# A graph-attention kernel: mask loads as 32-bit words on the sync queue, and a new order of units in the first and last batches

## The chip, the cores and the metric

One core of a Trainium2 chip runs the whole kernel. The metric is the device time of one launch in microseconds. Five engines matter: TensorE (PE; its weight loads are shown as PEld), VectorE (DVE), ScalarE (ACT), GpSimd (POOL) and SyncE (SP), which here only issues DMAs. Each engine executes its instructions strictly in the order in which the program gives them, and waits where an operand is not ready or a buffer is not free.

## What is computed

x is (16, 1024, 256) f32, adj is (16, 1024, 1024) int32 of zeros and ones. Two layers follow each other for each of the 16 batches; each is a pre-norm graph attention with a residual:

```python
h = jnp.maximum(_layernorm(x, axis=-1), 0.0)
x = x + _L0_gnn_ref(h, adj, ...)      # 4 heads of 64
h = jnp.maximum(_layernorm(x, axis=-1), 0.0)
x = x + _L1_gnn_ref(h, adj, ...)      # 8 heads of 32, biases on q, k, v

# inside a layer
scores = jnp.einsum('bhne,bhme->bhnm', Q, K) * scale
scores = jnp.where(adj > 0, scores, -jnp.inf)     # one mask for all heads
attn = jax.nn.softmax(scores, axis=-1)
out = concat_heads(attn @ V) @ Wo.T + bo
```

Everything is f32 on the chip.

## The kernel before, in words

Scores are computed transposed, keys on partitions and queries in columns, without subtracting a maximum; the sums of the exponentials are checked at the end (`test`, L288), and a flag computed from that check (`verdict`, L823) decides whether a slow, careful program runs instead. It does not run here.

**Steps.** The work is a list of 768 steps. A batch has two query halves (qh) of 512 queries. In layer 0 a half has two groups (pairs of heads) of 4 steps, in layer 1 two groups (four heads each) of 8 steps: 16 steps of layer 0 and 32 of layer 1 for a batch. A step is four 128 x 512 blocks. `scores` (L446) puts them on PE into two PSUM pairs out of a ring of three; `exponentials` (L461) masks each pair on DVE (L477) and takes the exponential on ACT (L483); `weigh` (L488), two steps later, multiplies by v on PE (L495). The list interleaves batches: layer 0 of batch b+1 (its first step is called a, `first[b+1]`) and then layer 1 of batch b (its first step is c = a + 16, `second[b]`).

**Order.** `Stream.run` (L541) writes every engine's program. In layer 0 it takes two steps at a time, in layer 1 one: scores of the new steps; then `weigh` of the steps two back and, in layer 1, their counting (`count_steps`); then counts that are due; exponentials; then the functions that are due at this step, first those without much PE work, last `turn`, `k`, `q`, `values`, `end_half`. `later(i, f)` makes f due at step i. All due steps are written out by hand (L766 to L819 and `end_group`), and functions that are due at one step go in the order in which they were entered; those of the hand-written list are entered before those of `end_group`.

**Sums.** In layer 0 `add_tiles` (L500) adds the exponentials' tiles on DVE and POOL (L504, L507, L508, L510). In layer 1 POOL adds the tiles of odd steps to those of even ones (L608), and `accumulate` (L591) adds two of the results by a DMA that POOL issues. `count` (L342) sums over the partitions with a matmul on ones, into a PSUM tile pz with one buffer. Then, some steps apart: `spread` (an ACT copy, L366, and four DMAs), `invert` (a DVE reciprocal and a DMA to DRAM, vd), `fetch` (DMAs back, inv), `normalize` (POOL, L406) and `end_half` (PE with wo, then x is added on DVE, L441; in layer 1 the result goes out, L444).

**Inputs.** `open_x` loads a half of x on SP into one of three buffers. `stats` (DVE), then two small POOL ops, `norm` (ACT, L214) and a transposition: for the first inputs `turn` on PE with the identity (L236), later `turn_blocks` (DVE, L240), `put_blocks` and `place_blocks` (SP, through DRAM). `k`, `q` and `values` are PE projections with a copy on ACT, DVE and ACT. `add_bias` (POOL, L223) adds the output's bias to x.

**Mask.** A batch's mask is 8 units of 128 queries x 1024 keys. `load` (L143) is a DMA on POOL's queue that turns int32 into bf16 (256 KB), into one of two buffers; `put` (ACT, L164) writes it as fp8, `flip` (DVE, L170) transposes it in 32 x 32 blocks. Four units are one half, and the first masking op of a half needs all four. `second` (ACT, L175) changes a unit for layer 1. For batch 0 the units are loaded into two tiles of the ring of the exponentials.

**Head and tail.** Before the first step the program loads weights and x, and does for both halves of batch 0 statistics, norm, turn, k, q, values, and four units of the mask (L676 to L717). At the end `finish` (L408) normalizes and writes the last half; six checks (L292) and `verdict` follow.

## Time and profile before

| what | us |
|---|---|
| median of three timed runs (3191.0 to 3192.33) | 3191.39 |
| the profiled execution's own time | 3184.43 |
| its span | 3182.7 |
| PE busy / DVE / ACT / POOL | 3119.6 / 2521.7 / 2236.4 / 2540.5 |
| adj loads: 128 issues on POOL, each on the engine | 1.62 |
| first scores of step 0 start at | 37.7 |
| step 16 / step 32 / step 64 start at | 116.7 / 210.0 / 333.5 |
| one batch in the middle (48 steps) | 194 |

A line of the timeline gives start, length, engine, line of the code, operation, what is written from what, how many, and in brackets the idle time of the engine before it with what ended it. A line of the waits gives engine and line, what was waited for, and us in total, number of times, and the longest.

### The profile page before, as it was taken

To read this page: it belongs to the slowest core of one execution; us is meant where nothing else is said; L and a number is where in the kernel's file an instruction comes from. 1 tells how busy PE (TensorE), PEld (TensorE's weight loads), DVE (VectorE), ACT (ScalarE), POOL (GpSimd) and SP (SyncE) were. 2 spreads that over 40 slices of the span, in tenths; PEclk is the share of its full clock that TensorE was granted. 3 is DMA by queue.
4 is the path that set the end of the run, shared out by engine and by line. 5 is a ranking of instruction groups with operands and counts; after the bars stand their busy time and mean duration, and the time that the engine had idled before them with its cause. 6 is when DMAs were issued, how large, how long until landed. Compare 5 with 4: busy or idle time off the path is not lost.

```text
span 3182.7 us, 45121 instructions
## 1 busy us (share of the span) xinstructions
PE 3119.6 (98%) x16662; PEld 1221.8 (38%) x16662; DVE 2521.7 (79%) x2882; ACT 2236.4 (70%) x2440; POOL 2540.5 (80%) x1358
## 2 busy tenths in 40 slices
PE   8989999999999999999999999999999999999998
PEld 3433333434334343333433334333343433434332
DVE  6678788887878878788887878878888787887776
ACT  5657767686676766767677686776768667676765
POOL 5568788797887978878788797878879788796776
PEclk9999999999999999999999999999999999999999
DMA  7216556364563745636355463555636446372421
GB/s 94 34 31 123 105 103 115 76 130 91 104 117 80 132 85 104 126 83 126 85 110 113 89 122 82 113 104 104 115 76 130 91 102 118 83 132 68 87 61 32
DMA packets 449684, 308.46 MB, mean 97 GB/s; under 512 B 248752, under 2 KB 408752, under 8 KB 432432
## 3 DMA queue, kind: packets, MB, share of 16 engines
q0 software_dynamic: 283344, 173.82, 33.8%
q1 hardware_dynamic: 166112, 131.68, 15.1%
q8 instruction: 133, 2.18, 0.3%
q14 instruction: 95, 0.78, 0.1%
HBM read 149.95 MB, written 47.96 MB: 62 GB/s over the span
## 4 chain that ended last, share of the span: by engine, by line
PE 79%; DMA 8%; DVE 7%; issue 2%; SPq 1%; POOL 1%; ACT 1%; DVEq 0%; POOLq 0%; ACTq 0%
PE ps L454 27%; PE po L495 23%; PE pq L270 11%; PE py L436 7%; PE pv L306 6%; PE pz L347 4%; DMA p<-p 4%; DVE p L477 3%; DMA out_dram<-x 3%; DMA x<-in_x_dram 1%; POOL p L608 1%; DVE p L507 1%; DVE st L195 1%; DVE p L504 1%; SPq L444 1%
## 5 line engine op out<-in xcount | busy, mean ns | idle before, releaser
L483 ACT ACTIVATE p<-p 128x1024 f32<-128x1024 f32 x1536 | 1613.0, 1056 | 722.0 <-DVE p L477 662.1
L477 DVE SCALAR_TENSOR_TENSOR p<-mask,ps 128x1024 f32<-128x1024 fp8e5 x1536 | 1786.2, 1214 | 373.8 <-PE ps L454 360.0
L608 POOL TENSOR_TENSOR p<-p,p 128x1024 f32<-128x1024 f32 x510 | 1217.8, 2449 | 135.9 <-PE po L495 115.8
L454 PE MATMUL ps<-qT,kT 32*128 32x512 f32 (+1 forms) x6144 | 1125.3, 628 | 19.7 <-DVE p L477 15.9
L495 PE MATMUL po<-p,v 128*32 128x512 f32 (+1 forms) x6144 | 981.0, 600 | 3.1 <-ACT cat L358 2.8
L454 PEld LDWEIGHTS ps<-qT,kT 32*128 32x128 f32 (+1 forms) x6144 | 380.8, 184 | 694.9 <-issue 288.8
L495 PEld LDWEIGHTS po<-p,v 128*32 128x32 f32 (+1 forms) x6144 | 233.6, 118 | 684.6 <-issue 468.2
L508 POOL TENSOR_TENSOR p<-p 128x1024 f32<-128x1024 f32 x128 | 302.5, 2363 | 89.0 <-DVE p L507 83.6
L507 POOL TENSOR_TENSOR p<-p,p 128x1024 f32<-128x1024 f32 x64 | 150.7, 2355 | 200.1 <-DVE p L504 120.3
L406 POOL TENSOR_TENSOR cat<-cat,inv 128x512 f32<-128x512 f32 x127 | 193.0, 1566 | 91.9 <-DMA inv<-vd 89.8
L270 PE MATMUL pq<-hT,wk 128*128 128x512 f32 x512 | 238.4, 609 | 2.7 <-DMA hT<-turned 1.6
L306 PE MATMUL pv<-wv,hT 128*128 128x256 f32 x1024 | 237.8, 385 | 0.1
L270 PE MATMUL pq<-hT,wq 128*128 128x512 f32 x512 | 236.6, 605 | 0.1
L436 PE MATMUL py<-wo,cat 128*128 128x256 f32 x1008 | 234.0, 385 | 1.2 <-DVE p L477 1.2
L306 PEld LDWEIGHTS pv<-wv,hT 128*128 128x128 f32 x1024 | 189.4, 190 | 72.1 <-DVE p L477 25.0
L436 PEld LDWEIGHTS py<-wo,cat 128*128 128x128 f32 x1008 | 186.6, 190 | 73.3 <-issue 35.1
L149 POOL DMA_DIRECT2D adj<-in_adj_dram x128 | 207.6, 1622 | 4.6 <-issue 4.0
L504 DVE TENSOR_TENSOR p<-p 128x1024 f32<-128x1024 f32 x128 | 171.0, 1336 | 0.0
L347 PE MATMUL pz<-p,ones 128*32 128x512 f32 x1248 | 163.4, 596 | 7.6 <-DMA p<-p 6.8
L592 POOL DMA_DIRECT2D p<-p x133 | 121.8, 916 | 53.1 <-POOL p L608 19.5
L441 DVE TENSOR_TENSOR x<-py,x 128x1024 f32<-128x1024 f32 x63 | 76.9, 1221 | 101.7 <-PE py L436 100.7
L223 POOL TENSOR_TENSOR x<-x,bo 128x1024 f32<-128x1024 f32 x64 | 156.9, 2512 | 0.0
(51 smaller groups left out, 1750.9 us busy)
## 6 DMA issues: line engine op xcount, KB each, us to landing
p<-p POOLq DMA_DIRECT2D x133, 1024.0 KB, 8.1
adj<-in_adj_dram POOLq DMA_DIRECT2D x128, 256.0 KB, 9.7
turned<-hn SPq DMA_DIRECT2D x58, 512.0 KB, 3.5
hT<-turned SPq DMA_DIRECT2D x232, 128.0 KB, 5.3
x<-in_x_dram SPq DMA_DIRECT2D x128, 128.0 KB, 2.8
inv<-vd SPq DMA_DIRECT2D x128, 128.0 KB, 2.9
inv<-vd SPq DMA_DIRECT2D x252, 64.0 KB, 4.8
out_dram<-x SPq DMA_DIRECT2D x124, 128.0 KB, 2.8
```

Source lines behind the costliest of these rows:

```text
L149: nc.gpsimd.dma_start(at, rows[u // 4, u % 4])
L270: nc.tensor.matmul(pq[:, m, :], wt[self.layer][:, c, ts(m, P)], self.hT[half][:, c, :], start=(c == 0), stop=(c == 1),)
L306: nc.tensor.matmul(pv[:, i, :], self.hT[half][:, c, ts(i, P)], w.v[self.layer][:, c, :], start=(c == 0), stop=(c == 1),)
L347: nc.tensor.matmul(self.s[ts(r, 32), :], w.ones.to_broadcast([P, 32]), of, start=start, stop=stop)
L436: nc.tensor.matmul(py[:, i, :], self.half.cat[:, c, ts(i, P)], w.o[self.layer][:, c, :], start=(c == 0), stop=(c == 1),)
L454: nc.tensor.matmul(st.ps[i // 2][:, i % 2, :], gr.inp.kT[r * D : (r + 1) * D, gr.g, ts(kt, P)], gr.inp.qT[gr.qh][r * D : (r + 1) * D, gr.g ...
L477: nc.vector.scalar_tensor_tensor(out=half, in0=gr.mask.m[gr.qh][:, kt // 4, :, kt % 4].unsqueeze(1).to_broadcast([P, 2, 512]), scalar=-EDG ...
L483: nc.scalar.activation(half, half, AF.Exp, scale=gr.scale)
L495: nc.tensor.matmul(gr.o[r * D : (r + 1) * D, :], gr.inp.v[:, kt, h * D : (h + 1) * D], st.halves[i // 2][:, i % 2, :], start=(kt == 0), st ...
L504: nc.vector.tensor_add(a, a, b)
L508: nc.gpsimd.tensor_add(a, a, b)
L608: nc.gpsimd.tensor_add(half, half, of)
```

## The change

1. `Mask.load` is issued on SP, into an int32 tile (512 KB); the mask buffers are one instead of two (the same bytes). `put` reads int32. Loads, puts and flips come at other steps: four units of a batch in the layer-0 steps a+8 to a+14, one at a+45, three at the beginning of the next 16 steps; a load stands directly behind the put of the unit before it; a flip two steps behind its put (one for unit 4).
2. Head: the identity is multiplied 16 times by itself into a PSUM tile that nobody reads. SP's order is x, wk and wq, x, four mask units, wv, four units, x of batch 1, the other weights. The steps begin after k and q of the first half, turn of the second and the first four mask units; k(1), values(0) and values(1) come at step 0, q(1) at step 2, add_bias at 10 and 12.
3. The inputs of batch 1 are due at slightly other steps, the second half of x of batch b+2 is opened at c (before at a+14), and its first statistics are at c+2 (before at c).
4. The first group of layer 1 accumulates at once instead of two steps later.
5. Last batches: other steps for `second`, for the inputs of the last layer, and for the first count of the last batch; the two tests that were at the very end come seven steps (or 37) after their group.
6. The two small tiles of `verdict` come from the pool of constants instead of a pool opened at the end.

```diff
-    adjp = ctx.enter_context(tc.tile_pool(name="adjp", bufs=2))
+    adjp = ctx.enter_context(tc.tile_pool(name="adjp", bufs=1))
...
-                at = adjp.tile([P, 4, 256], BF16, tag="adj", name=f"adj_{self.b}_{u}")
+                at = adjp.tile([P, 4, 256], I32, tag="adj", name=f"adj_{self.b}_{u}")
...
-            nc.gpsimd.dma_start(at, rows[u // 4, u % 4])
+            by.dma_start(at, rows[u // 4, u % 4])          # by=nc.sync
...
-                    self.later(i + 2, gr.count, one, j == 1, st.last)
+                    self.later(i + (4 if j == 1 and not (gr.qh or gr.g) else 2), gr.count, one, j == 1, st.last)
...
-                    if gr.qh or gr.g:
-                        self.accumulate(one, gr.one)
-                    else:
-                        self.due.setdefault(i + 2, []).insert(0, (self.accumulate, (one, gr.one)))
+                    self.accumulate(one, gr.one)
...
-                self.later(i + k if gr.inp.b + gr.layer < B - 1 else len(self.steps) + 2, gr.inp.test)
+                self.later(i + k, gr.inp.test)
...
+    warm = psum_pair("warm")
+    for _ in range(16):
+        nc.tensor.matmul(warm[:, 0, :P], w.ident, w.ident, start=True, stop=True)
+    open_w(2)
+    open_x(0, 1)
+    for u in range(4):
+        load(u)
+    open_w(1)
+    for u in range(4, NT):
+        load(u)
+    open_x(1, 0)
+    open_w(6)
+    open_x(1, 1)
+    open_w(len(loads))
     inp.stats(0)
     inp.norm(0, whole=True)
     inp.stats(1)
     inp.turn(0)
+    inp.norm(1, whole=True)
+    mask.put(0)
     inp.k(0)
+    mask.put(1)
     inp.q(0)
     inp.turn(1)
+    for u in range(4):
+        if u > 1:
+            mask.put(u)
         mask.flip(u)
...
+    for i, f, half in (0, inp.k, 1), (0, inp.values, 0), (0, inp.values, 1), (2, inp.q, 1):
+        later(i, f, half)
+    for half in range(QH):
+        later(10 + 2 * half, inp.add_bias, half)
...
-        for i, u in zip((0, 1, 2, 3, 4, 6, 8, 10), range(NT)):
+        for i, u in zip((0, 2, 4, 6, 7, 9, 11, 13), range(NT)):
             later(a + i, masks[b].second, u)
...
-            later(a + 14, open_x, b + 2, 1)
+            later(c, open_x, b + 2, 1)
...
-                norms(other, 1, c, c + 4, c + 5, c + 6, bias=c + 36)
+                norms(other, 1, c + 2, c + 4, c + 5, c + 6, bias=c + 36)
...
-            for i, t in zip((9, 13, 17, 22, 33, 37, 41, 45), range(NT)):
-                later(a + i - 5, mask.load, t)
-                later(a + i, mask.put, t)
-                later(a + i + 1, mask.flip, t)
+            at = 6, 8, 10, 12, 14, 45, 49, 51, 53
+            for t in range(NT):
+                later(a + at[t], mask.load, t)
+                later(a + at[t + 1], mask.put, t)
+                later(a + at[t + 1] + (1 if t == 4 else 2), mask.flip, t)
...
-            block_inputs(last, 0, c + 10, c + 11, c + 12, c + 14, c + 16, c + 20)
-            norms(last, 1, c + 13, c + 14, c + 16, c + 17)
-            block_inputs(last, 1, c + 18, c + 19, c + 20, c + 24, e + 6, e + 4)
-            for u in range(NT):
-                later(c + 8 + 2 * u, masks[b + 1].second, u)
+            block_inputs(last, 0, c + 10, c + 11, c + 12, c + 16, c + 20, c + 24)
+            norms(last, 1, c + 13, c + 16, c + 20, c + 21)
+            block_inputs(last, 1, c + 22, c + 23, c + 24, c + 28, e + 8, e)
+            for i, u in zip((4, 5, 8, 12, 16, 20, 24, 28), range(NT)):
+                later(c + i, masks[b + 1].second, u)
...
-    row = work.tile([P, 1], F32, tag="row", name="row")
+    row = w.row
...
-    bad = work.tile([1, 1], I32, tag="bad", name="bad")
+    bad = w.bad
```

(e = c + 32 is the first step of the last batch's layer 1.)

## The prediction

> **What bounds the kernel now.** I read the page first, then PE's waits, over the whole span and over the long middle, then timelines where these waits fall.
>
> ```profile
> PE 3119.6 (98%) x16662; PEld 1221.8 (38%) x16662; DVE 2521.7 (79%) x2882; ACT 2236.4 (70%) x2440; POOL 2540.5 (80%) x1358
> ...
> PE 79%; DMA 8%; DVE 7%; issue 2%; SPq 1%; POOL 1%; ACT 1%; DVEq 0%; POOLq 0%; ACTq 0%
> ```
>
> TensorE is the bound, and the change removes no matmul. Only 3182.7 - 3119.6 = 63 us of idle PE (and a few us at a low clock) can be won. PE's waits (us in total, times, longest), whole span:
>
> ```profile
> PE ps L454 <- DVE p L477: 15.9, 18, 2.1
> PE ph L236 <- ACT hn L214: 13.2, 5, 10.3
> PE pz L347 <- DMA p<-p: 6.8, 13, 1.2
> PE tot L831 <- DVE row L829: 6.4, 1, 6.4
> PE po L495 <- ACT cat L358: 2.8, 3, 2.2
> ...
> PE pq L270 <- DMA hT<-turned: 1.6, 1, 1.6
> ```
>
> and between 260 and 3120 us:
>
> ```profile
> PE ps L454 <- DVE p L477: 9.8, 14, 0.8
> PE pz L347 <- DMA p<-p: 6.8, 13, 1.2
> ```
>
> So a batch in the middle (194 us) loses just two stalls, 0.75 and 0.52 us. With a the first layer-0 step of a batch and c = a + 16, the first sits at step c+3 and the second at c+11, in each of 13 batches. The timeline of the first, in batch 3:
>
> ```profile
> 800.47 1.75 SPq L135 DMA_DIRECT2D x<-in_x_dram  x4
> 802.26 0.43 SPq L389 DMA_DIRECT2D vd<-vn  x1
> 804.70 0.43 DVE L195 BATCH_NORM_STATS2 st<-x 128x6 f32<-128x256 f32 x1 [2.11 <-DMA x<-in_x_dram]
> 808.84 3.91 POOL L406 TENSOR_TENSOR cat<-cat,inv 128x512 f32<-128x512 f32 x2 [5.74 <-DMA inv<-vd]
> 809.51 2.11 DVE L507 TENSOR_TENSOR p<-p,p 128x1024 f32<-128x1024 f32 x1
> 812.80 1.13 PE L454 MATMUL ps<-qT,kT 32*128 32x512 f32 x4 [0.74 <-DVE p L477]
> ```
>
> The x load of step a+14 holds SP 6.3 us, until 800.47 (SP's own waits name the out DMA of that buffer). The normalizer's vd, ready at 797.0, queues behind it; POOL gets inv 5.74 us late; its multiply then lies on top of DVE's L507, which takes 2.11 us where it takes 1.23 alone (at 748.84); the next masking op frees its PSUM pair late. Head and tail:
>
> ```profile
> 10.26 2.80 PE L236 MATMUL ph<-ident,hn 128*128 128x128 f32 x8 [10.26 <-ACT hn L214]
> 14.16 5.56 PE L270 MATMUL pq<-hT,wk 128*128 128x512 f32 x8 [1.10 <-ACT hT L237]
> 19.55 3.60 PE L270 MATMUL pq<-hT,wq 128*128 128x512 f32 x8
> 54.20 1.13 PE L454 MATMUL ps<-qT,kT 64*128 64x512 f32 x4 [2.01 <-DVE p L477]
> 3175.74 0.22 DVE L829 TENSOR_REDUCE row<-chk 128x1 f32<-128x64 f32 x1 [3.40 <-DMA out_dram<-x]
> ```
>
> **Head.** Until 24.0 us PE does the same work in the same order: turn(0), k(0), q(0), turn(1), here without values(0) between. First the masks: SP now issues eight 512 KB loads behind x, wk, wq, x. In 0:40 the hardware queue moved 4.46 MB in 53% of 40 us, 210 GB/s; seven half-MB transfers to the fourth mask end near 2 + 17.5 = 19.6 us, the first mask at 12. ACT's order is norm(1) to 16.2, put(0) 1.15 to 17.4, kT copy 19.75-20.8, put(1) to 21.9, hT copy (1.0) after turn(1), 25.1, put(2), put(3) to 27.4; DVE flips the last (0.45) by 28.0. So no mask load is late, and the first masking op (L477) starts at 28.0 instead of 38.9. PE meanwhile waits: 0.4 for the qT copy (23.2 + 1.2), then three score pairs fit PSUM and the fourth waits from 27.65 to 29.2, 1.55; together 2.0. k(1), values(0), values(1) follow at 30.4 (10.3 us, covering DVE and ACT, which finish at 34), scores of steps 2 and 3 at 40.7, and from there PE has q(1) and the projections of batch 1 to put beside DVE. Before, the stretch after 37.7 lost 0.8 (8.10 for 32 score matmuls against 2 x 3.63), 2.01, 1.04 (0.45, 0.16, 0.43) and 1.7 (clock 0.50 for 3.41 us at 55.5), 5.5. Gain 5.5 - 2.0 = 3.5. From below: all of 5.5; from above: a loss of 3, if DVE still falls behind and the clock halves again (2.0 + 1.7 more than taken).
>
> The 16 identity matmuls: a 128x512 product is two rows of 0.45, so a 128-column one is 0.22, 16 are 3.5 us at full and 7 at half clock. They start when the identity is made, 1.5, end by 8.5, and PE idles to 10.26 as before. The 2.01 us idle above was enough for the clock to halve, so I take 0; if the clock held, 0.8 of turn(0) (its last rows come from ACT at 11.7) and 2.1 of the k group would go, -2.9.
> The Trainium skill ("TensorE: Matmul & The Clock Gate", Part 1) has a free-running activity window of some 3.4 us: a mostly idle window halves the clock. By it the 1.8 us or more to 10.26 lose the warmth in some window phases and keep it in others, 0 or -2.9; the 3.41 us at 0.50 in this trace agree with the window's length.
>
> **Batches 0 and 1 (80-265 us), 12 us of stalls.** Two stalls of 0.26 and 0.43 at 193-195 us come from a mask put ahead of the kT copy (192.9); it moves one due slot earlier and clears, -0.7. The 1.19 at 265 is POOL's queue: adds, accumulate, two multiplies, add_bias, adds; the bias (2.4) moves 30 steps on and the mask load issue (1.6) leaves: -1.2. A flip (0.43) joins the overloaded DVE at a+7: +0.4. The 2.1 us stalls at 160, 208 and 217 have their causes (statistics, qT copy, norm) left where they are. Net -1.5, between -4 and +3.
>
> **Middle, 13 batches.** (1) x half 1 opens at c instead of a+14, statistics at c+2. In SP's place now stands mask load 4, which waits for put(3) on ACT. The exponentials end at 797.7, put at 798.8, so vd goes at 799.3 instead of 802.3, less some 1 to 2 us for following half a MB. DVE's 2.11 wait goes. L507 then meets the multiply wholly, partly or not; of 0.75 I take 0.45, ends 0 and 0.75. (2) The accumulate of the first layer-1 group is issued with its adds (end 829.9), not behind the next adds (837.9). Landing takes 8.1, so it is there at 839 for a count at 846: all of 0.52 goes. POOL idles 829.9-833.3, so the issue (0.9) is free. (3) 8 loads a batch leave POOL, 8 x 1.62 = 13 us, and enter SP, 8 x 0.45 of issue, SP being mostly idle. POOL is not the bound: 0 itself. (4) Puts and flips: the same number, moved. ACT's tight iterations gain 1.05 each: 6-7 has 1.6 us free before its next exponential, 10-11 1.67, 14-15 1.66. DVE's flip at a+7 takes 0.35 of 0.92 free; at a+3 and a+5 there are 1.7 and 3.6. So 0, held for +0.15 a batch. (5) SP's order: each load t+1 stands behind put t, at the end of an ACT iteration; sums wait for ACT's copy anyway; the fetch at a+8 starts some 3 us later, its multiply at 775.8 moves to about 778, before the next POOL add at 780.2. One buffer instead of two: a load has an iteration (7.2 us or more). (6) put now reads four bytes an element; ACT's exponential reads f32 in 1.06 for as many columns, put takes 1.14 from bf16, so 1.14 stays. In DMA time a load falls: 8 loads were 72.2% of 40 us in the head (3.6 us each on all engines), on the hardware queue 0.52 MB at 210 GB/s is 2.5; DMA was 50% busy, so 0. Sum 13 x (0.45 + 0.52 - 0.15) = 10.7, between -16.5 and +6.
> The Trainium skill ("DMA: Bandwidth & Descriptors", Queues, rings and completion order) speaks against (5): descriptors of one queue are taken in ring order, so small vd and inv transfers now wait behind mask bytes that lay on another queue. No row before shows it; with 210 GB/s it would be 2.5 us on a chain that has won 3, and (1) would give 0: 13 x 0.45 = 6 us less gain.
>
> **Last batch, 5.4 us of stalls** (2.22, 1.56, 0.20, 0.21, 0.44, 0.80 between 2976 and 3077). The second mask pass (1.1 on ACT each) starts four steps earlier and is spread; k, q, v of half 0 go 2 to 4 steps later, so hT (late by 1.56) is there; the first pair's count goes two steps later, past the copy of the sums it waited 0.80 for. The moved projections (k(1), q(1), v(1)) are PE work either way. I take -3.5, ends 0 and -5.4.
>
> **Tail.** row and bad leave a pool that took over the x buffer: L829 no longer waits for the out DMA. Four of six L292 (0.24 each) go earlier, so bad is done at 3172.3, not 3176.43. Then loads of the flag (0.5), PE's branch (4.37) and 1.1 of ending follow: 3178.6 for 3182.7, -4.1. SP issues out DMAs to 3174.1 and has its own chain of about 3.5, ending 3177-3178, just beside. Ends -1 and -4.5.
>
> **Sum**, against the profiled execution (3184.43: span 3182.7 and 1.7 around it): -3.5 - 1.5 - 10.7 - 3.5 - 4.1 = -23.3, 3161.1. The median of the runs, 3191.39, is 7.0 above the profiled one; the same gain gives **3168.1**.
>
> **Rivals.** (B) The middle's stalls stay or others of the same size replace them: only ends gain, -12.6, 3179. For: L507 is late by overlap, which a 2 us shift may not end; against: the second stall has a plain cause. (C) The clock holds from the identity matmuls and the middle wins both stalls: -30, 3161. (D) Slower: mask load 0 lands late. It is issued near 763.9, behind x and beside hT; put(0) stands in ACT ahead of the po copy (L358), which PE needs at 775.2. Up to 9.6 us of landing cost nothing, then PE loses one for one in each of 14 batches; (23.3 + 6.4)/14 = 2.1, so it decides from 11.7 us. At 12.5 it costs 41 us, 3209. For: mask loads landed in 9.7 on POOL's queue (18.5 in the head); against: 512 KB of turned on SP lands in 3.5. (E) No change to be measured: new ACT, DVE or SP lateness of about 1.5 us a batch, 3188. For: 70 to 98% full iterations in layer 0.
>
> **Numbers.** Forecast 0.47 (3158 to 3177), C 0.10, B 0.18, E 0.13, D 0.12. Faster by over 0.2% (6.4 us, about what a measurement can tell from none): 0.75; within: 0.13; slower: 0.12. The range leaves out D and the tips: 3158 to 3191.
>
> **What would show it.** First L477 near 28 us; k matmuls after 14 us at 0.85 or 0.45 each (clock); the waits of PE without "pz <- DMA p<-p" and with "ps <- DVE p" under 8 us; vd issued before x at c; L829 without a DMA wait. Wrong: ACT's put (L164) waiting for "DMA adj" in layer 0, new stalls repeated every 194 us.

## The result, and the profile after

The changed kernel takes 3428.22 us (median of four runs, 3419.01 to 3435.93) where the kernel before takes 3191.19 (3190.60 to 3192.33): 1.074 times as long, with a 95% interval of 1.071 to 1.077. I had forecast 3168.1 and a range up to 3191. The profiled execution of the changed kernel has a span of 3417.2 us, 234.5 more than the 3182.7 before.

The page of the changed kernel, the line of busy times and the chain of work that ended last (shares by engine, then by line):

```profile
PE 3191.7 (93%) x16694; PEld 1243.8 (36%) x16694; DVE 2531.5 (74%) x2882; ACT 2236.8 (65%) x2440; POOL 2311.5 (68%) x1230
...
PE 53%; DMA 26%; SPq 6%; DVE 6%; POOL 4%; issue 3%; ACT 3%; DVEq 0%; POOLq 0%; ACTq 0%
PE ps L456 17%; PE po L497 15%; DMA adj<-in_adj_dram 10%; PE pq L272 8%; PE py L438 7%; DMA vd<-vn 6%; DMA p<-p 4%; DVE p L479 4%; PE pz L349 3%; PE pv L308 3%; POOL p L610 2%; DMA inv<-vd 2%; DMA x<-in_x_dram 2%; SPq L137 2%; DMA sums<-s 1%
```

TensorE was 79% of the chain and DMA 8%; now they are 53% and 26%, and one tenth of the span is the mask's loads. PE's idle time went from 63.1 us to 225.5 (+162.4), and its busy time rose by 72.1 although only the 16 small products were added. Most of that second part is the clock. The trace's clock records (each gives a stretch and the share of TensorE's full clock granted in it) have 196.6 us at half clock, before 23.1, and PE was busy for 137.4 us of that, before for 10.3; half of this difference is 63.6 us, and the products took some 6. Idle and busy time together are the 234.5. The two largest waits of PE, and the mask's line of ACT's waits, in the changed kernel (engine, line, what was waited for; us in total, times, longest):

```profile
PE ps L456 <- ACT v L312: 90.3, 13, 8.5
PE ps L456 <- DVE p L479: 49.7, 20, 8.9
```

```profile
ACT mask L166 <- DMA adj<-in_adj_dram: 326.0, 96, 10.8
```

and the same line in the kernel before:

```profile
ACT mask L164 <- DMA adj<-in_adj_dram: 3.7, 1, 3.7
```

Before, ACT waited for a mask load once, now 96 of 128 times. It is the sign that the prediction named for being wrong. Where it hurts is seen in the timeline of batch 3 (its a begins at 768.1), SP's queue first, then ACT, then PE:

```profile
816.28 0.63 SPq L151 DMA_DIRECT2D adj<-in_adj_dram  x1
821.31 1.21 SPq L391 DMA_DIRECT2D vd<-vn  x1
827.46 0.61 SPq L151 DMA_DIRECT2D adj<-in_adj_dram  x1
```

```profile
826.28 1.15 ACT L166 ACTIVATE mask<-adj,numbers 128x1024 fp8e5<-128x1024 int32 x1 [6.77 <-DMA adj<-in_adj_dram]
827.34 0.57 ACT L360 COPY cat<-po 128x512 f32<-128x512 f32 x1
827.80 1.15 ACT L177 ACTIVATE mask<-mask,numbers 128x1024 fp8e5<-128x1024 fp8e5 x1
828.85 1.00 ACT L312 COPY v<-pv 128x1024 f32<-128x1024 f32 x1
...
837.93 1.15 ACT L166 ACTIVATE mask<-adj,numbers 128x1024 fp8e5<-128x1024 int32 x1 [1.95 <-DMA adj<-in_adj_dram]
```

```profile
823.43 1.99 PE L456 MATMUL ps<-qT,kT 64*128 64x512 f32 x8
829.90 2.08 PE L456 MATMUL ps<-qT,kT 64*128 64x512 f32 x4 [4.48 <-ACT v L312]
```

Mask load 0 is issued at 816.28 and `put` starts with it at 826.28, 10.0 us later. ACT stands idle for 6.77 of these. Behind the put in ACT's order lie the copy of po, a second mask pass and, last, the copy of v out of PSUM (the memory that PE writes to); the next scores need that PSUM pair and wait 4.48 us. The clock records have half clock from 829.88 on, for 3.41 us. `put` empties the one buffer, so load 1 goes at 827.46, and its put starts 10.5 us later: the loads alternate with the puts, one after another.

Time between the starts of the steps' scores, mean of 12 middle batches, worked out from the trace (a is the first layer-0 step, c = a + 16; only rows that differ by over 0.3 us somewhere; the other kernels are those of the experiments):

| steps | before | after | load in four parts | before, x at c | last kernel |
|---|---|---|---|---|---|
| a+2 to a+4 | 10.85 | 12.07 | 10.85 | 10.85 | 10.85 |
| a+4 to a+6 | 11.99 | 15.20 | 11.99 | 11.99 | 11.99 |
| a+10 to a+12 | 7.22 | 16.78 | 8.23 | 7.22 | 7.22 |
| c to c+2 | 9.36 | 9.78 | 9.36 | 9.36 | 9.36 |
| c+2 to c+4 | 9.81 | 7.65 | 7.66 | 7.72 | 7.66 |
| c+4 to c+6 | 8.64 | 13.23 | 8.67 | 8.64 | 8.70 |
| c+6 to c+8 | 8.40 | 7.63 | 7.63 | 7.63 | 7.63 |
| c+10 to c+12 | 6.10 | 5.36 | 5.36 | 6.07 | 5.36 |
| c+12 to c+14 | 7.65 | 8.26 | 8.24 | 7.65 | 8.21 |
| whole batch | 194.41 | 210.38 | 192.37 | 191.51 | 191.36 |

The places of loss in "after" are those of the mask: the puts of units 6 and 7 (steps a+3 and a+5), put(0) at a+8, which stops a+10, and c+4, where x is late. There the mask's load is the cause at one remove. In batch 4, SP's queue:

```profile
1071.04 0.62 SPq L151 DMA_DIRECT2D adj<-in_adj_dram  x1
1071.76 1.87 SPq L391 DMA_DIRECT2D vd<-vn  x1
1079.67 2.42 SPq L400 DMA_DIRECT2D inv<-vd  x4
1082.18 1.95 SPq L137 DMA_DIRECT2D x<-in_x_dram  x4
```

vd is 8 KB, but its readers wait until 1079.67, 6 us after its issue has ended; x stands behind them, DVE's statistics wait for x until 1087.07, and the scores wait 1.34 us for DVE. Over the whole run SP waited for vd 318.5 us in 54 places (5.9 each), before 160.3 in 84 (1.9 each).

**How fast is such a load?** A stretch of the changed kernel's trace in which nothing but one mask load is in flight, 840.5 to 846.5 us (packets, megabytes, share of 16 engines):

```profile
DMA packets 484, 0.49 MB, mean 82 GB/s; under 512 B 1, under 2 KB 484, under 8 KB 484
...
q1 hardware_dynamic: 484, 0.49, 25.1%
```

25.1% of 16 engines are 4.02 engines: one load is served by four engines, at 82 GB/s, however idle the others are. 0.52 MB take 6.4 us at that rate; from the issue to a put that waits for it pass 8.2 us at the least and 10.0 in the median of the 96. The load's source is written with four dimensions, `k r g c`, and k, the slowest, has 4 values.

The Trainium skill ("DMA: Bandwidth & Descriptors", "Why a DMA increments its semaphore by 16 and not by 1") has a rule that fits: a DMA uses the largest number of engines, up to 16, that divides the slowest dimension of both its sides; with 4 and 128 that is 4. The trace's 4.02 agrees.

### The profile page after: what moved, and what is told of

Read it like the earlier page. It is cut to its first block, busy times and chain, and to the rows that moved or that the text cites. A ratio compares the mean times of both kernels' runs of the same rounds, so it can differ in the third digit from the quotient of the medians.

```text
span 3417.2 us, 45104 instructions
## 1 busy us (share of the span) xinstructions
PE 3191.7 (93%) x16694; PEld 1243.8 (36%) x16694; DVE 2531.5 (74%) x2882; ACT 2236.8 (65%) x2440; POOL 2311.5 (68%) x1230
## 4 chain that ended last, share of the span: by engine, by line
PE 53%; DMA 26%; SPq 6%; DVE 6%; POOL 4%; issue 3%; ACT 3%; DVEq 0%; POOLq 0%; ACTq 0%
PE ps L456 17%; PE po L497 15%; DMA adj<-in_adj_dram 10%; PE pq L272 8%; PE py L438 7%; DMA vd<-vn 6%; DMA p<-p 4%; DVE p L479 4%; PE pz L349 3%; PE pv L308 3%; POOL p L610 2%; DMA inv<-vd 2%; DMA x<-in_x_dram 2%; SPq L137 2%; DMA sums<-s 1%
## 5 line engine op out<-in xcount | busy, mean ns | idle before, releaser
L456 PE MATMUL ps<-qT,kT 32*128 32x512 f32 (+1 forms) x6144 | 1163.6, 640 | 174.0 <-ACT v L312 90.3
L408 POOL TENSOR_TENSOR cat<-cat,inv 128x512 f32<-128x512 f32 x127 | 166.2, 1314 | 327.0 <-DMA inv<-vd 296.0
L166 ACT ACTIVATE mask<-adj,numbers 128x1024 fp8e5<-128x1024 int32 x128 | 146.8, 1148 | 326.0 <-DMA adj<-in_adj_dram 326.0
L438 PE MATMUL py<-wo,cat 128*128 128x256 f32 x1008 | 247.3, 401 | 7.7 <-DVE p L479 7.5
L438 PEld LDWEIGHTS py<-wo,cat 128*128 128x128 f32 x1008 | 196.0, 200 | 92.3 <-DVE p L479 31.9
L506 DVE TENSOR_TENSOR p<-p 128x1024 f32<-128x1024 f32 x128 | 198.0, 1547 | 0.9 <-PE po L497 0.9
L349 PE MATMUL pz<-p,ones 128*32 128x512 f32 x1248 | 170.8, 617 | 24.3 <-DMA p<-p 24.3
L197 DVE BATCH_NORM_STATS2 st<-x 128x6 f32<-128x256 f32 x256 | 108.2, 423 | 92.1 <-DMA x<-in_x_dram 87.6
L443 DVE TENSOR_TENSOR x<-py,x 128x1024 f32<-128x1024 f32 x63 | 77.2, 1225 | 122.7 <-PE py L438 122.5
```

Of the source, the lines that this page charges most:

```text
L349: nc.tensor.matmul(self.s[ts(r, 32), :], w.ones.to_broadcast([P, 32]), of, start=start, stop=stop)
L408: nc.gpsimd.tensor_mul(o, o, inv)
L438: nc.tensor.matmul(py[:, i, :], self.half.cat[:, c, ts(i, P)], w.o[self.layer][:, c, :], start=(c == 0), stop=(c == 1),)
L456: nc.tensor.matmul(st.ps[i // 2][:, i % 2, :], gr.inp.kT[r * D : (r + 1) * D, gr.g, ts(kt, P)], gr.inp.qT[gr.qh][r * D : (r + 1) * D, gr.g ...
L506: nc.vector.tensor_add(a, a, b)
```

## The experiments

Theory A: the load is slow because it is one DMA on four engines; all else follows from puts that wait. Rivals: it is slow because it shares SP's queue with other transfers (B), or because it is int32, twice the bytes (C), or because of one buffer or the order of loads and puts (D).

### The load in four parts

```diff
-            by.dma_start(at, rows[u // 4, u % 4])
+            for k in range(4):
+                by.dma_start(at[ts(k, 32)], rows[u // 4, u % 4][k])
```

Same bytes, queue, buffer and steps; the slowest dimension of each part is 32.

> The changed kernel with each mask load issued as four DMAs of 32 partitions (128 KB) instead of one of 128 partitions; bytes, buffers, steps and queue as they are. Theory A (few DMA engines): with nothing else in flight the load moves 81 packets of 1 KB a us at 53 ns each, so 4.3 engines work, and the outermost dimension of its source has 4 entries; with 32 entries all 16 work. Then a load lands in 3 to 4 us, ACT's wait for adj falls from 326 us to under 20, and the kernel takes 3165 to 3180 us. Theory B (one buffer and SP's order: a load stands behind the put of the unit before it and behind other transfers): the waits stay, and the time stays over 3390 us, with 384 more issues on SP.

Measured: 3158.01 us (3155.12 to 3159.24), 0.991 of the kernel before on the same chip (0.989 to 0.993), and 270 us less than the changed kernel. Its ACT wait, the landing of a part on the page, and the window 795.25 to 798, in which the parts of a load (and one 8 KB vd) are in flight:

```profile
ACT mask L167 <- DMA adj<-in_adj_dram: 25.6, 13, 2.7
```

```profile
adj<-in_adj_dram SPq DMA_DIRECT2D x512, 128.0 KB, 3.0
```

```profile
DMA packets 681, 0.52 MB, mean 190 GB/s; under 512 B 178, under 2 KB 681, under 8 KB 681
...
q1 hardware_dynamic: 681, 0.52, 61.7%
```

61.7% are 9.9 engines, 190 GB/s instead of 82. ACT's wait falls from 326.0 us to 25.6, the half-clock time from 196.6 to 32.7, PE's waits for `ACT v` are gone, and those for `DVE p` fall from 49.7 us to 10.7. Theory A stands. B, C and D alone are not enough for the loss: queue, bytes, buffer and order are those of the changed kernel.

### The same number of DMAs, but four engines each

```diff
-            by.dma_start(at, rows[u // 4, u % 4])
+            for g in range(4):
+                by.dma_start(at[:, g, :], rows[u // 4, u % 4][:, :, g, :])
```

Cut along g, so that k stays the slowest dimension.

> The same number of DMAs as in e1_split_k (four of 128 KB for a load), but cut along the other dimension: each has all 128 partitions, and the outermost dimension of its source still has 4 entries. Theory A: the same 4 engines carry all four, a load still lands in 8 to 10 us, and the time is that of the changed kernel, 3415 to 3450 us. Theory C (a single DMA of 512 descriptors is slow as such): smaller DMAs land sooner, and the time falls to that of e1_split_k.

Measured: 3328.71 us in one run (before 3188.51). The window 827 to 831 and the waits:

```profile
DMA packets 364, 0.36 MB, mean 91 GB/s; under 512 B 10, under 2 KB 364, under 8 KB 364
...
q1 hardware_dynamic: 364, 0.36, 25.6%
```

```profile
ACT mask L167 <- DMA adj<-in_adj_dram: 231.0, 71, 8.7
```

The part on the engines is right: 25.6% are 4.1 engines, so it is the shape and not the number of DMAs that decides. The time is not: it lies 140 us above before, but 100 below the changed kernel, which theory A did not expect. From the issue of a load's first part to a put that waits for it pass 9.1 us in the median, 0.9 less than in the changed kernel; SP's wait for vd is smaller (273.1 us instead of 318.5) and so is PE's for p<-p (7.5 instead of 24.3). Whether small transfers get in between the four parts wasn't tried; these 100 us stay open.

### Loads on POOL's queue again, with the new steps

```diff
-        def load(self, u, at=None, by=nc.sync):
+        def load(self, u, at=None, by=nc.gpsimd):
```

once with bf16 tiles and two buffers, as before (the lines for the tiles are left out here), and once with int32 and one buffer.

> The changed kernel with mask loads as before: bf16 on POOL's queue with two buffers; steps of loads, puts and flips, head and last batches as changed. Theories A and B: the 7% are all in the load, so the time falls to 3170 to 3185 us. If the new steps of the units themselves are at fault, it stays over 3300 us.

> The changed kernel with its 32-bit loads and its one buffer, issued on POOL's queue instead of SP's. Theory A: POOL's queue has used all engines for the same shape before (its loads of this shape did not hold ACT up), so the time falls under 3200 us although the buffer is single. Theory B (one buffer): the alternation of put and load stays and the time stays over 3300 us.

Measured: bf16 3293.06 us, 1.033 of before (1.031 to 1.035); int32 3450.5 in one run. I had expected both to be near or below the kernel before, and both are far above. The landing in the kernel before, then the lines of landing and of ACT's wait, bf16 and then int32:

```profile
adj<-in_adj_dram POOLq DMA_DIRECT2D x128, 256.0 KB, 9.7
```

```profile
adj<-in_adj_dram POOLq DMA_DIRECT2D x128, 256.0 KB, 10.9
```

```profile
ACT mask L166 <- DMA adj<-in_adj_dram: 185.8, 69, 6.3
```

```profile
adj<-in_adj_dram POOLq DMA_DIRECT2D x128, 512.0 KB, 11.6
```

```profile
ACT mask L166 <- DMA adj<-in_adj_dram: 267.0, 81, 7.4
```

So the load was never fast: POOL's loads landed in 9.7 us before, and land here in 10.9 (256 KB) and 11.6 (512 KB). That POOL's queue had used all engines, as I had assumed for the int32 kernel, no run shows. The kernel before hid it. Its loads were issued five steps ahead of the put, and the distance from issue to put was never under 11.7 us (median 17.8). With the new steps a load goes directly behind the put of the unit before it: in the bf16 kernel ACT had to wait for 69 loads, and without its wait it would have been there 9.7 us after the issue (median of the 69). Before PE loses, the order of the change leaves load 0 some 5 us (worked out below), and only a load in four parts lands in about that. Theory D is half right: with slow loads, the new order is what makes them felt.

Two more things make these kernels slow, so they are no pure test of the load. In both, POOL issues the mask loads ahead of its statistics in the head (shown in the next experiment), and step 16 starts at 134.3 and 139.0 us, against 115.0 with the four parts on SP. And with one buffer POOL itself stands at a load until the put has emptied the buffer: 268.8 us in 72 places in the int32 kernel, while the bf16 kernel's POOL waits less than 7 us ahead of its loads. What the buffer and what the bytes have of the 157 us between the two was not separated.

### POOL's loads two iterations ahead

```diff
-                later(a + at[t], mask.load, t)
+                later(a + (at[t - 1] if t else 4), mask.load, t)
```

on the bf16 kernel.

> e3_pool_bf16 (mask loads as bf16 on POOL's queue, two buffers, else as changed: 3293 us) with each load issued two iterations before its put instead of one. Theory: a load in this shape takes 9 to 11 us on either queue, and the changed order gives it one layer-0 iteration (7.2 us and more); with two it is there. ACT's wait for adj (186 us) falls under 15, and the time to 3160 to 3180. If the moved puts and flips or the loads' share of POOL are at fault, the time stays over 3270.

Measured: 3228.86 us, 1.012 of before (1.010 to 1.014). ACT's wait:

```profile
ACT mask L166 <- DMA adj<-in_adj_dram: 22.6, 6, 6.5
```

185.8 us of it went to 22.6, with the same slow loads, and 64 us of time with it: the lead is what counts. But I had expected it below the kernel before, and it is 38 above. The step table names two places. One is the head: step 16 starts at 133.3 us instead of 116.7. No put there waits for a load. POOL does its work in order, and its small statistics op stands behind all eight load issues:

```profile
3.58 9.22 POOL L151 DMA_DIRECT2D adj<-in_adj_dram  x6
18.26 1.54 POOL L151 DMA_DIRECT2D adj<-in_adj_dram  x1 [5.46 <-issue]
19.82 1.05 POOL L205 TENSOR_TENSOR rstd<-ve,numbers 128x4 f32<-128x4 f32 x1
```

DVE's part for it was ready at 8.23; so PE's first transposition starts at 21.84 instead of 10.26. The other place is a+14 to a+16, 10.77 us instead of 7.22 in each batch, where PE's scores wait for DVE's addition of x (L443, 27.3 us in 14 places). In batch 3 POOL's multiply waits 5.06 us for inv, until 814.61; POOL's adds come behind it, DVE's masking op waits 7.91 us for them, and x's addition stands behind that. Why inv is late in this kernel I have not settled.

### The identity matmuls: none, 16 and 30

On the kernel with four parts: without the 16 products, and with 30 of them.

```diff
-    for _ in range(16):
+    for _ in range(30):
```

> e1_split_k (3158 us) without the 16 identity matmuls. In e1's trace they end at 7.6, PE is then idle for 2.5 us, the clock is halved from 9.7 to 20.0 us, and the first 8 k matmuls take 6.62 us. Theory: they win nothing; without them the clock rises within the k matmuls as before the change (full from 17.9), the first scores start at 23 to 26 us, and the time is within 3 us of e1's share of the kernel before (0.9908). Rival: they hold the clock in most executions, and without them 3 us are lost.

> e1_split_k with 30 identity matmuls instead of 16, so that they last to where the first transpositions start (10 to 11 us). Theory: without the idle 2.5 us the clock stays full from about 6 us on, the first 8 k matmuls take 3.6 to 3.8 instead of 6.62 us, the first scores start at 21.5 to 23 instead of 25.5, and the kernel gains 2 to 3 us on e1. Rival: the clock halves all the same, and only PE's queue gets longer (0 to +1 us).

Measured: none 3154.96 us, 0.989 of before (0.987 to 0.990); 30 3150.45, 0.987 (0.986 to 0.989); 16 had 0.991 (0.989 to 0.993). Step 16 starts at 114.1, 111.5 and 115.0 us. The timelines of the head, with 16 and with 30 (three groups each):

```profile
1.54 6.09 PE L686 MATMUL warm<-ident 128*128 128x128 f32 x32 [1.54 <-POOL ident masks.py:199]
10.13 2.80 PE L239 MATMUL ph<-ident,hn 128*128 128x128 f32 x8 [2.50 <-ACT hn L217]
14.04 6.62 PE L273 MATMUL pq<-hT,wk 128*128 128x512 f32 x8 [1.10 <-ACT hT L240]
```

```profile
1.54 9.91 PE L686 MATMUL warm<-ident 128*128 128x128 f32 x60 [1.54 <-POOL ident masks.py:199]
11.29 1.05 PE L239 MATMUL ph<-ident,hn 128*128 128x128 f32 x8
13.44 3.70 PE L273 MATMUL pq<-hT,wk 128*128 128x512 f32 x8 [1.10 <-ACT hT L240]
```

With 16, PE idles 2.50 us before the first real work, the clock records show half clock from 9.7 to 20.0 us, and the products with wk take 6.62 us, longer than the 5.56 of the kernel before. With 30 the clock does not fall in the head, they take 3.70, and the first scores start at 22.0 instead of 25.5. Sixteen products win nothing; what counts is that they reach up to the real work.

The Trainium skill ("TensorE: Matmul & The Clock Gate", Part 1) gives a window of about 3.4 us after which the clock is set; the records at half clock here are 3.41 us long and multiples of it, except where a program ends in one, which agrees. The page speaks of an idle window; here PE was busy for 1.32 of the 3.41 us before 9.72, and for 1.40 of those before 55.48 in the kernel before, and the clock halved both times.

### One part of the change alone: x opened at c

The kernel before, with two lines of part 3 only:

```diff
-            later(a + 14, open_x, b + 2, 1)
+            later(c, open_x, b + 2, 1)
...
-                norms(other, 1, c, c + 4, c + 5, c + 6, bias=c + 36)
+                norms(other, 1, c + 2, c + 4, c + 5, c + 6, bias=c + 36)
```

> The kernel before with one part of the change: the second half of x of batch b+2 is opened at c instead of a+14, and its first statistics are at c+2 instead of c. Prediction's step: SP no longer stands at that x load while vd waits, so the steps c+2 and c+3 of a middle batch (9.81 us together before, 7.66 in e1_split_k) fall to 9.0 or less, and 13 batches win 6 to 28 us; the stall of pz at c+11 may stay. If the stall comes from the overlap of DVE and POOL alone, the two steps stay at 9.8.

Measured: 3147.14 us in one run, 44 below the 3190.70 of the kernel before on that chip; the middle gains 2.90 us a batch (c+2 to c+4 2.09, c+6 to c+8 0.77). In this kernel's SP queue vd and inv go ahead of x:

```profile
792.96 0.34 SPq L389 DMA_DIRECT2D vd<-vn  x1
796.67 2.40 SPq L398 DMA_DIRECT2D inv<-vd  x4
799.19 1.95 SPq L135 DMA_DIRECT2D x<-in_x_dram  x4
```

and the scores of c+3 come without a wait:

```profile
807.88 1.22 PE L454 MATMUL ps<-qT,kT 32*128 32x512 f32 x8
```

The same group in the kernel before:

```profile
812.80 2.26 PE L454 MATMUL ps<-qT,kT 32*128 32x512 f32 x8 [0.74 <-DVE p L477]
```

Only 0.74 of what was lost there stood in the idle list; another 1.04 stood inside the busy time of that group, whose second half waited too, and 0.77 came at c+6. My prediction had read 0.75 from the idle column. This one part gives 0.986 of the kernel before in its one run, and the last kernel below, with every part and fast loads, 0.984: nearly all that was won here lies in these two lines.

### One part alone: accumulating at once

The kernel before, with part 4 only:

```diff
-                    if gr.qh or gr.g:
-                        self.accumulate(one, gr.one)
-                    else:
-                        self.due.setdefault(i + 2, []).insert(0, (self.accumulate, (one, gr.one)))
+                    self.accumulate(one, gr.one)
```

> The kernel before with one part of the change alone: the first group of layer 1 accumulates at once instead of two steps later. My prediction's step (2): PE's wait for the DMA that accumulates (6.8 us in 13 places) goes and nothing takes its place, the steps c+10 to c+14 take together 13.0 to 13.3 us instead of 13.75 and the time is some 6.8 us less, about 3182. Theory from the run with the mask loads in four parts: the counts only move, steps c+10 to c+12 fall from 6.10 to 5.36 and c+12 to c+14 rise from 7.65 to about 8.2, a batch loses 0 to 0.2 us less, and the time is the same within 3 us.

Measured: 3189.29 us in one run, against 3189.63. c+10 to c+12 falls from 6.10 to 5.36 and c+12 to c+14 rises from 7.65 to 8.12; the batch is 194.36 instead of 194.41. Of the 0.74 won, 0.47 is lost again at the next steps, as the second theory has it; another 0.33 comes at c+2 (10.14 instead of 9.81), which it had not foreseen and which I have not traced. Nothing is won.

### One part alone: the verdict's tiles

The kernel before, with part 6 only (`row = w.row`, `bad = w.bad`).

> The kernel before with one part of the change alone: the two small tiles of the flag's computation come from the pool of constants. My prediction's step (tail, ends -1 and -4.5): L829 has no DMA wait and PE's branch comes earlier; the four early tests are not in this kernel, so the part is at most 3.4 us, the wait of L829 on the out DMA before, and the stretch from the last step's scores to the end falls from 29.1 to about 25.7 us; everything before it stays, 3188. Rival: the program ends with SP's chain (its last out DMA issue at 3174.1 and about 3.5 us behind it), so less than 1.5 us of that is seen, and the stretch stays above 27.6.

Measured: 3181.09 us in one run, against 3189.63. From the last scores to the end 24.5 us instead of 29.1. The checks of the sums end at 3172.21 in this kernel; DVE's next row:

```profile
3172.24 0.22 DVE L830 TENSOR_REDUCE row<-chk 128x1 f32<-128x64 f32 x1
```

The reduction follows the checks at once, where it waited 3.40 us for the out DMA before. The tail's gain of the whole change, 3.8 to 3.9 us, is no larger than this part's, 4.6. The 1.2 us beyond the wait come from the clock: in the kernel before a half-clock record of 3.41 us begins at 3165.0 and the last 14 products with wo take 4.95 us; here no such record lies there, and they take 3.60.

### The last batch, and the first half of x

The four-part kernel lost 3.4 us between step 704 and the last step's scores where I had forecast a gain of 3.5. On the kernel with 30 products, the last batch's order of before was put back (steps of the last inputs, of `second` and of its first count):

```diff
-                    self.later(i + (4 if j == 1 and not (gr.qh or gr.g) else 2), gr.count, one, j == 1, st.last)
+                    self.later(i + 2, gr.count, one, j == 1, st.last)
...
-            block_inputs(last, 0, c + 10, c + 11, c + 12, c + 16, c + 20, c + 24)
-            norms(last, 1, c + 13, c + 16, c + 20, c + 21)
-            block_inputs(last, 1, c + 22, c + 23, c + 24, c + 28, e + 8, e)
-            for i, u in zip((4, 5, 8, 12, 16, 20, 24, 28), range(NT)):
-                later(c + i, masks[b + 1].second, u)
+            block_inputs(last, 0, c + 10, c + 11, c + 12, c + 14, c + 16, c + 20)
+            norms(last, 1, c + 13, c + 14, c + 16, c + 17)
+            block_inputs(last, 1, c + 18, c + 19, c + 20, c + 24, e + 6, e + 4)
+            for u in range(NT):
+                later(c + 8 + 2 * u, masks[b + 1].second, u)
```

and a second kernel has besides

```diff
-            later(a + 6, open_x, b + 2, 0)
+            later(a + 7, open_x, b + 2, 0)
```

so that mask load 0 goes ahead of x on SP's queue.

> The kernel with the mask loads in four parts and 30 identity matmuls, with the last batch as in the kernel before (steps of the second mask pass, of the last layer's inputs and of its first count). Theory, from the step table: the changed order of the last batch costs 4 us (layer 1 of it, steps 704 to 736, took 118.5 us instead of 114.5), where my prediction had a gain of 3.5. So 114.5 again and 3146 to 3147 where the kernel with 30 matmuls had 3150.5. Rival, my prediction's step: the new order is right and the 4 us have another cause (the second pass's place, kept early for the batch before), then the stretch stays at 118 or becomes longer, and the time is 3150 to 3154.

> As the kernel with the last batch's old order, and in every middle batch the first half of x is opened at a+7 instead of a+6, so that on SP's queue mask load 0 goes ahead of it. Theory: what still waits in the middle is put(0) for load 0 (ACT, 13 times, 25.6 us), because the load stands behind a x load that waits for its buffer; with the load ahead of it, steps a+10 to a+12 fall from 8.23 to 7.22 in 14 batches, the wait of ACT on adj falls below 8 us, and the time is 13 us below that of the kernel with the last batch's old order: 3131 to 3136. Rival: x is now late by a place in the queue and its statistics (a+10 in the due list) hold DVE, so the 1.0 us comes back in steps a+12 to c; then the time stays within 3 us of the other kernel.

Measured: 3155.05 us, 0.989 (0.987 to 0.990), and 3140.75, 0.9842 (0.9825 to 0.9858). The stretch from step 704 to the last became longer, 224.9 and 227.0 us, after 221.0 with the new order and 216.6 before (227.0 is from an execution of 3149.01 us, the slowest of its four). Steps 704 to 736 took 117.7 us with the old order put back and 117.8 with the new one, so the 114.5 of before did not come back: my explanation fell. The rival's sign is there, a stretch that becomes longer; the cause that it names was not tested. The step on x is right: a+10 to a+12 is 7.22 again, the batch is 191.33 us instead of 192.25, and ACT waits for a mask load only twice in the second kernel, 1.2 us together. The time is 14 us below that of the first, about the 13 expected; it is above the 3131 to 3136 named, as the first did not win its own 4 us.

Then the changed last batch again, with x at a+7; and the same with the projection q of the second half of batch 14's layer-1 input (batches count from 0, so the last but one) back at c+6:

```diff
-            block_inputs(mine, 1, a, a + 6, a + 7, c, c + (6 if b + 2 < B else 8), c + 2)
+            block_inputs(mine, 1, a, a + 6, a + 7, c, c + 6, c + 2)
```

> The mask loads in four parts, 30 identity matmuls, the first half of x at a+7 behind mask load 0, and the last batch in the changed order. Theory: the step period is 191.3 us as in the run with the old last batch, from step 704 to the last step 221 us instead of 227, and the time 3136 to 3139 us. Rival: the order of the last layer's inputs and of its second mask pass does not matter, and the time is 3139 to 3143.

> The same, with the projection q of the last batch's first-layer output's second half at c+6, where the kernel before had it, instead of c+8. Theory: at c+6 to c+8 the kernel with the change has too little work on PE beside a burst of masking and statistics on DVE; PE then waits 0.73 us for DVE's masking op just ahead of q, and in that window the clock halves for 3.4 us. With q back at c+6 the six steps c+6 to c+12 take together 20 to 20.5 us (before 20.09, 7.63 + 4.94 + 7.52) instead of 21.7 (5.12 + 11.24 + 5.36), no half-clock record lies there, and the stretch from step 704 to the last is 218 to 219. The time is 2 to 3 us lower. Rival: the stall only moves behind q, to the next group of scores (the row of the kernel before with x opened at c has 9.17 there), and the stretch stays at 221.

Measured: 3139.40 us, 0.985 (0.983 to 0.987), and 3136.75 (3135.94 to 3137.83), 0.9843 (0.9826 to 0.9859). In the first the stretch is 220.7 us instead of 227.0, as its theory has it, but against the kernel before it is no faster than the kernel with the old order, 0.9842; so the rival, that the order does not matter for the time, is not excluded. With q at c+6 the steps c+6 to c+12 take 20.10 us, as the theory says, but c+12 to c+14 then takes 12.59, and the stretch is 219.7 instead of 220.7, not 218 to 219: the rival is nearer, the stall moves behind q. In the last kernel, PE's waits between step 704 and the last step are 2.2 us for ACT's copy of po and 2.0 and 1.2 for DVE's masking op. They are 5.4 us, as many as before (5.4), in other places; a clock record of 3.4 us at half speed lies among them (at 2940.0), which costs 1.7 and is not there before. The remaining 1.4 of the 3.1 us stay open. This kernel has the shortest time of all, 1.6% below the kernel before. Between 330 and 2860 us its PE waits at one place of the batch only, at the product with wo for DVE's masking op, 12 times and 6.1 us together.

## Why the prediction was wrong

By stages, in us of the profiled executions (the rows add up to the change of the span):

| term | forecast | changed kernel | load in four parts |
|---|---|---|---|
| head, to step 16 | -3.5 | +17.6 | -1.7 |
| batches 0 and 1, to step 64 | -1.5 | +1.4 | -0.6 |
| middle, 64 to 688 | -10.7 | +210.2 | -26.6 |
| 688 to 704 | 0 | +4.7 | 0.0 |
| last batch, 704 to the last scores | -3.5 | +4.4 | +3.4 |
| tail | -4.1 | -3.8 | -3.9 |
| sum | -23.3 | +234.5 | -29.4 |

**The step that failed is (5) and (6) of the middle**, "a load has an iteration (7.2 us or more)" and "0.52 MB at 210 GB/s is 2.5". The rate of 210 GB/s is 4.46 MB in 53.0% of the first 40 us, from this line of the kernel before:

```profile
q1 hardware_dynamic: 5584, 4.46, 53.0%
```

The 53.0% are a share of all 16 engines, so 210 GB/s is what they move when all of them work, as with several transfers in flight. A single load had four of them: it got 82 GB/s, and its put began no sooner than 8.2 us after the issue where it waited for it (median 10.0), while PE begins to lose after about 5.7 us of landing of load 0 (below). The row nearest to it was in the profile, the 9.7 us in which the very same source pattern landed on POOL's queue, and I put it down to that queue. The cheaper comparison, the 3.5 us of 512 KB of turned on SP, was a store of another shape. With the load in four parts the stage's other terms show, and their sum, -29.4, lies near the -23.3 forecast partly by luck: the middle won 26.6 instead of 10.7, and the last batch lost 3.4 where it was to win 3.5.

**Rival D** was the right mechanism (load 0 late, put(0) in ACT's way, in every batch) with a chance of 0.12 and a wrong threshold. The load was issued 10.9 us after the start of a+6, as assumed (10.4). But the first reader that PE misses is not the po copy: the scores of a+11 need the PSUM pair that the v copy (L310) empties, which stands behind put, po copy and a second mask pass. In the kernel before PE begins these scores at 773.4. Going back by 1.0 for the copy, 1.15 for the pass, 0.57 and 1.15 for copy and put gives a put at 769.6, so 5.7 us of landing are free, not 9.6. By that, 10.0 us cost 4.3, and the stall in batch 3 is 4.48. The mean stall is 6.9 (90.3 in 13), and the halved clock makes 9.56 us of step a+10 from it. D's price also had one place in a batch; there are four (the rows of the step table at a+2, a+4, a+10 and c+4), and it had no term for the clock.

**Head.** The four-part kernel follows the forecast: first masking op at 28.69 us (28.0 forecast), k(1) at 31.1 (30.4), scores of step 2 at 41.63 (40.7). In the changed kernel the same slow load breaks it: "seven half-MB transfers to the fourth mask end near 19.6" used 210 GB/s again, and the last flip before the first masking op is at 33.85, not 28, and the masking op starts at 34.41. The loads hold SP as well: forecast was 0.45 us of SP for an issue, but of the eight mask loads of the head six take SP 4.3 to 5.9 us each, and wv, issued between them, 5.31. In the kernel with four parts each issue takes 0.6. SP's first four loads and wv, then DVE:

```profile
5.53 15.92 SPq L151 DMA_DIRECT2D adj<-in_adj_dram  x4
21.49 5.31 SPq L670 DMA_DIRECT2D wv<-in_wv_dram  x1
```

```profile
33.85 0.45 DVE L172 STREAM_TRANSPOSE mask<-mask 128x256 f32<-128x256 f32 x1 [5.41 <-ACT mask L166]
```

The forecast of 0 for 16 identity matmuls holds, and so does its reason, that PE idles before the first real work.

**Term (1), x at c**, was right in its cause and too small: 0.45 a batch forecast, 2.9 measured alone, since the idle list shows only 0.74 of that loss and another 1.04 lay inside a group that counts as busy. **Term (2), accumulating at once**, 0.52 forecast, is 0.05 alone: the wait moves on. **The page that spoke against (5)** (small transfers taken in ring order behind mask bytes) fits what is seen where the load is slow, 5.9 us for each wait for vd instead of 1.9, and much less with four parts, 2.4 (124.8 us in 52); that ring order is the reason, no run shows by itself. **Last batch:** the causes were read rightly, but each stall removed came up at another place, so -3.5 was 3.4. **Tail:** -4.1 forecast, -3.8 to -4.6 measured, of which the wait for the out DMA is 3.4.

## What to carry to other kernels

Before a DMA is moved to a place with little slack, look how many engines one such DMA alone keeps busy: a stretch of the trace with nothing else in flight gives its rate, and the rate of a busy stretch does not. Where the pattern's slowest dimension is small, cut the DMA along it; here that alone was worth 270 us. A slow load that nobody waits for is found by the distance from its issue to its reader, and this distance is what a new order spends; the slack is counted to the first reader that the bound engine misses, with all that lies between on the waiting engine. And an idle list understates a stall that falls between the matmuls of one group.

## What the runs showed of the hardware

- One DMA of 512 KB with a slowest dimension of 4 kept 4.0 of 16 engines busy (82 GB/s); cut along that dimension into four, 9.9 (190 GB/s); cut along another, 4.1.
- A load on POOL's queue that turns int32 into bf16 took about as long (10.9 us) as one that copies int32 (11.6), though it writes half the bytes.
- For a full clock at the first real products, PE work had to reach up to them: a pause of 2.5 us after six of work was followed by 10 us at half clock, and with no pause the first scores came 3.5 us earlier.
- The stalls of the changed kernel (the longest 8.9 us) cost in clock about 0.4 of what they cost in waiting: PE's busy time at half clock rose from 10.3 to 137.4 us, which is 63.6 us more than at full clock, beside 162.4 of additional idle time.
- In the head an issue on SP took mostly 4.3 to 5.9 us behind 512 KB loads on four engines, and 0.6 behind the same loads in four parts: a slow load also holds what is issued after it.
